# Projections of an attention layer: pair 0's operands put by in the pauses of the tiles, longer pauses, routing in smaller steps, two weight sums one product earlier

## The chip, the cores and the metric

The kernel runs on one core of a Trainium2 chip. The metric is the device time of one execution in microseconds (us), lower is better. The core has five engines that run side by side, each with its own queue: PE (matrix products), DVE (vector work), ACT (activations and copies), POOL (vector work without access to the matmul results) and SP, which here only issues DMA transfers. An engine takes its instructions in order: one that waits holds up everything queued behind it.

## The reference

Inputs are float32: hidden states x of 4 batches x 512 rows x 1024, attention weights w_qkv (1024 x 6144) and w_o (4096 x 1024), and the weights of a feed-forward part with routed low-rank additions.

```python
xn   = layernorm(x)
qkv  = xn @ w_qkv                        # 32 heads of 128, 8 key/value heads
attn = softmax(q k^T * D**-0.5 - slope * sqrt(distance), causal)
x = x + (attn v) @ w_o                   # attention
      + xn @ W.T + b                     # feed-forward
      + low_rank_r(xn) * weight          # ranks r = 8, 16, 32, 64; the best of 4 by a gate
# gate: probs = softmax(xn @ gate_w.T + gate_b); r = argmax(probs); weight = top / top
```

## The kernel before, in words

The big products are done by Strassen's scheme in Winograd's form, twice over: seven outer products i in the order 1, 2, 6, 3, 7, 4, 5 (`PROJECTED`), each of seven inner products m1 to m7 of four matmuls. That saves matmuls and costs sums: sums of activations, sums of weights, sums of results.

The change lies in `project()`, the first 580 us or so, which makes q, k and v. The batches form two pairs. The products are done in *sets*, each of 512 columns of w_qkv: a set of keys and values (kv) and two of queries (q, q), four times over for pair 0 (kv0, q0, q1, kv2, ... q7: 12 sets), then the same for pair 1. `item(st, i)` is one outer product of one set. Its inner products come in the order m1, m5, the m4 of the item before, m6, m3, m2, m7. Results are taken out of the matmul banks by DVE (L130), and some of them (of products 1 and 5) by copies on ACT (L168). Other work is spread between the inner products: after each of them `beside()` takes steps from queues of Python generators, and a generator's `yield` ends a step. The queues are

- `weights`: `outer_w`, the outer sums of a set's weights (L508; the record has them under the helper's line L133) on DVE. Three homes `to0`, `to1`, `to2` hold results; the rest is done in place.
- `soon`: sums of activations that are needed next.
- `later`: work with no near due time, one step every `pace[1]`-th inner product (4 at first, then 3, from the third set on 2). In order: a pause of 9 steps, `routing(0)`, `routing(1)`, seven `put_by` of pair 0, then eight `tile_of_second`, with `routing(2)` after the fourth and `routing(3)` after the eighth.
- `apart`: three generators `weights_put_by`, which prepare sums of the weights of later stages: ACT issues a load into a buffer `wr` (L757, L764), a pause of 8 steps, four sums on POOL or DVE, a pause of 4, then SP stores the buffer (L799).

`put_by(i)` (pair 0) stores the operands of outer product i to DRAM for a later stage: four stores s<-x of 256 KB (L451) and one s<-xi of 768 KB (L453), five steps for each i, 35 in all, all issued by SP. `tile_of_second(t)` treats 128 rows of the second pair: a load of x (L693), a pause of 5 steps, layernorm statistics on DVE (L255, L258, L262, L265) and the normalising on ACT (L260 table load, L266), transposes on PE (L271), a product with the low-rank and gate matrices, stores; for the second batch of the pair further loads (L719), a pause of 4 steps, and four sums. `routing(bi)` turns the gate's results of one batch into a mask, with DVE instructions of a few numbers a partition: the softmax (L300 to L311), the weight (L316, L317, L321), for each of three further ranks a maximum (L325, two of three), a comparison (L328) and a product (L329), then four products with the low-rank results (L333); after that PE transposes them (L346), POOL sets a row of ones (L348) and ACT copies them out.

PE and SP issue in a hand-written order throughout `project()` (`manual_schedule`), DVE and POOL from the fifth product of the second set (k == 1, i == 5) on; before that, and for ACT throughout, the framework's scheduler orders the instructions. At the end of product 1 of the last set of pair 0 (q7), `flush(later)` runs what is left in `later` at once, because from there on the activations of pair 1 take the places of pair 0 (`hand_over`).

Of the kernel before, what the change touches and what calls it, by code (L numbers as in the profile page):

```python
# [65 lines left out]
def kernel(  # L66
# [225 lines left out]
    def route(bi):  # L292
        u = us.pop(bi)
        shape = [P, NT, NR]

        def small(tag, n=NR):
            return stats.tile([P, NT, n], F32, tag=tag, name=f"{tag}_{bi}", bufs=1)

        lg, pr, red, inv, top = small("lg"), small("pr"), small("red", 1), small("inv", 1), small("top", 1)
        nc.vector.tensor_tensor(  # L300
            lg, u[:, :, RMAX:], gb.unsqueeze(1).to_broadcast(shape), ALU.add
        )
        nc.vector.tensor_reduce(red, lg, AX.X, ALU.max)
        nc.vector.tensor_tensor(lg, lg, red.to_broadcast(shape), ALU.subtract)
        nc.scalar.activation(pr, lg, AF.Exp)
        yield
        yield
        nc.vector.tensor_reduce(red, pr, AX.X, ALU.add)
        nc.vector.reciprocal(inv, red)
        nc.vector.tensor_tensor(pr, pr, inv.to_broadcast(shape), ALU.mult)  # L310
        nc.vector.tensor_reduce(top, pr, AX.X, ALU.max)  # L311


        yield
        wgt = small("wgt", 1)
        nc.vector.reciprocal(wgt, top)  # L316
        nc.vector.tensor_tensor(wgt, top, wgt, ALU.mult)  # L317


        msk, best = small("msk"), small("best", 1)  # L320
        nc.vector.tensor_copy(msk[:, :, 0:1], wgt)  # L321
        for s in range(1, NR):
            prev = pr[:, :, 0:1] if s == 1 else best
            if s > 1:
                nc.vector.tensor_tensor(  # L325
                    best, pr[:, :, 0:1] if s == 2 else best, pr[:, :, s - 1 : s], ALU.max
                )
            nc.vector.tensor_tensor(msk[:, :, s : s + 1], prev, top, ALU.is_lt)  # L328
            nc.vector.tensor_tensor(msk[:, :, s : s + 1], msk[:, :, s : s + 1], wgt, ALU.mult)  # L329
            yield  # L330
        lo = 0
        for s, hi in enumerate(RANKS):
            nc.vector.tensor_tensor(  # L333
                u[:, :, lo:hi],
                u[:, :, lo:hi],
                msk[:, :, s : s + 1].to_broadcast([P, NT, hi - lo]),
                ALU.mult,
            )
            lo = hi
        return u  # L340
# [11 lines left out]
    def project(attention):  # L352
# [5 lines left out]
        with pool("a") as sb, tc.tile_pool(name="stats", bufs=2, reuse_waits="tile") as stats:  # L358
# [137 lines left out]
            def outer_w(st):  # L496
                w = W[st]
                q = [w[:, i * HC : (i + 1) * HC, ts(j, HS)] for i in range(2) for j in range(2)]
                n = f"{st[1]}{st[0]}_{st[2]}"

                t = [buf(f"to{i}", f"to{i}_{n}") for i in ((1, 2, 0) if st == sets[1] else range(3))]
                t.insert(2, q[1])
                TO[st] = {3: q[3]}
                for i, k, u, v in (
                    (5, 0, q[1], q[0]), (6, 1, q[3], t[0]), (7, 2, q[3], q[1]), (4, 3, q[2], t[1])
                ):
                    for c in range(0, HC, 2):
                        sub(nc.vector, t[k][:, c : c + 2], u[:, c : c + 2], v[:, c : c + 2])  # L508
                        yield
                    TO[st][i] = t[k]  # L510

            def raw_w(st, i):
                w = W[st]
# [74 lines left out]
                )  # L588


            soon, later, weights = deque(), deque(), deque()
            apart = (deque(), deque(), deque())
            pace = [1, 4, 0, False, 0, 0]


            delayed = []
# [92 lines left out]
            def tile_of_second(t):  # L689

                bi, i = divmod(t - 2 * NT, NT)
                xr = flat(r4(f"xin_{t}"))
                nc.sync.dma_start(out=xr, in_=xf[:, t, :])  # L693
                yield from pause(5)
                yield from normalise(xr, xr, t)
                xn = xr
                yield
                yield
                xt = flat(r4(f"xt_{t}")).rearrange("p (c k) -> p c k", k=P)
                for half in range(2):  # L700
                    transposed(bank, xn, t, half, xt[:, half * HC : (half + 1) * HC, :])
                    yield
                yield
                low_rank(bank, t, lambda c: xt[:, c, :])

                def to(j, x):
                    nc.sync.dma_start(out=xo_d[j][:, :, ts(i, P)], in_=x)

                low, high = xt[:, :HC], xt[:, HC:]
                if bi == 0:  # L710
                    yield
                    to(1, low)
                    to(2, high)
                    yield
                    return

                xf_t = flat(r4(f"xb_{t}")).rearrange("p (c k) -> p c k", k=P)
                for j in range(2):
                    nc.sync.dma_start(  # L719
                        out=xf_t[:, j * HC : (j + 1) * HC], in_=xo_d[1 + j][:, :, ts(i, P)]  # L720
                    )
                to(4, high)
                yield from pause(4)
                add(V, high, low, high)
                yield
                sub(V, low, xf_t[:, :HC], low)
                yield
                sub(V, xf_t[:, :HC], high, xf_t[:, :HC])
                to(5, high)
                yield  # L730
                sub(V, xf_t[:, HC:], xf_t[:, HC:], xf_t[:, :HC])
                yield
                to(7, low)
                to(6, xf_t[:, :HC])
                yield
                to(3, xf_t[:, HC:])
                yield
# [69 lines left out]
            def pause(n):  # L807
                for _ in range(n):
                    yield

            def hand_over(a, b, i):


                soon.append(pause(2))
                soon.append(once(b.take, i))
                at = PROJECTED.index(i)
                if at:
                    soon.append(b.inner(PROJECTED[at - 1], V))
                if i == 5:
                    soon.extend([pause(6), b.inner(5, V)])  # L820
                    for j in OUTER:
                        later.append(b.put_by(j))
# [4 lines left out]
            def stream():  # L827
# [41 lines left out]
                for j in (3, 7, 4, 5):  # L869
                    if j in (3, 7):  # L870
                        soon.append(a.outer(j, (V, V, V, V)))
                    soon.append(a.inner(j, GP if j == 4 else V))
                later.extend(a.put_by(j) for j in OUTER)
                for t in range(2 * NT, 4 * NT):
                    later.append(tile_of_second(t))
                    if t % NT == NT - 1:
# [3 lines left out]
                for k, st in enumerate(sets):  # L880
                    if k + 1 < len(sets) and sets[k + 1] not in W:

                        in_while(4, lambda k=k: W.update({sets[k + 1]: load_w(sets[k + 1])}))
                    if k > 1:
                        weights.append(outer_w(st))
                    pace[5] = pace[2]

                    pace[1] = 3 if k < 3 else 2
                    for i in PROJECTED:
                        if k < 2 and i < 3:  # L890
                            continue
                        need(pairs[st[0]], i)
                        if i > 2:
                            need_w(st, i)
                        if k == 0 and i == 5:
                            weights.append(outer_w(sets[1]))

                        pace[3] = k > 0 and k not in (NS - 1, NS)

                        pace[4] = pace[2] + {1: 0, 5: 4}.get(i, 9)  # L900
                        if k == len(sets) - 1 and i == 3:
                            done_first.__exit__(None, None, None)
                            attention()
                        nxt = PROJECTED[PROJECTED.index(i) + 1 :][:1]
                        if nxt:
                            in_while(4, lambda st=st, j=nxt[0]: ahead(st, j))
                        elif k < len(sets) - 1:
                            in_while(4, lambda k=k: ahead(sets[k + 1], 1 if k else 6))
                        yield item(st, i, accs[st])
                        if k == NS - 1:  # L910
                            if i == 1:
                                flush(later)
                            hand_over(a, b, i)
                        if k == 1 and i == 5:
                            pace[0] = 1
                            in_order.__enter__()
                    del W[st], TO[st]
# [1 line left out]
            run(stream(), beside)  # L919
            release(0)  # L920
            in_order.__exit__(None, None, None)
            assert not (soon or later or weights or any(apart))


    def attend(front, begin):
# [737 lines left out]
```

## Time and profile before

| | |
|---|---|
| runs | 2672.40, 2672.93, 2676.59 us; median 2672.93 |
| profiled execution | 2674.55 us, of it the profile's span 2672.8 |
| mean granted clock of PE | 0.994 |
| PE busy | 2606.5 us (98%), 11872 matmuls |
| DVE busy | 1785.0 us (67%) |
| ACT busy | 651.9 us (24%) |
| POOL busy | 1921.2 us (72%) |
| DMA | 656.19 MB, mean 246 GB/s |

PE is busy 98% of the span, so what counts is where it stands still. The page gives the share of each engine; the chain that ended last is followed back from the last instruction to what released it. In a timeline each row has a start, a length, the engine, the line and the operation with the tile that it writes and those that it reads, and in brackets the engine's idle time before it with what ended it. In a table by stretches each engine's busy time stands with its count of instructions; PEclk is the clock that PE was granted and the DMA share is that of the core's 16 DMA engines (it can pass 1 where packets overlap).

### The profile page before, as it was taken

The page shows a single profiled execution, that of the slowest core. Times are in us where ns is not written, and L with a number is a line of the kernel's source. Part 1 is how long each engine was busy: PE and PEld are TensorE (multiplying, and loading weights), DVE is VectorE, ACT ScalarE, POOL GpSimd, SP SyncE. Part 2 cuts the span into 40 slices and gives each one's busy share as a digit, 9 for nine tenths or more (in the row PEclk, how much of TensorE's full clock was granted, in tenths as well). Part 3 has the DMA queues.
Part 4 walks back from the last instruction along what each step waited for, and adds up shares of the span by engine and source line. Part 5 has one row for each costly group of instructions (what it writes and reads, how often), then busy time and mean ns, then how long its engine had stood idle before and what let it go on. Part 6 is the DMA issues. An engine that isn't in the chain of part 4 may idle for free.

```text
span 2672.8 us, 36000 instructions
## 1 busy us (share of the span) xinstructions
PE 2606.5 (98%) x11872; PEld 2079.8 (78%) x11872; DVE 1785.0 (67%) x3646; ACT 651.9 (24%) x1730; POOL 1921.2 (72%) x1984
## 2 busy tenths in 40 slices
PE   7899999999999999999999999999999999999999
PEld 7787878888888888866666666665888888888887
DVE  6876676787676667566766666666665566656574
ACT  3011111100000000177666666675000000000000
POOL 2687787877888889667777778676675566756583
PEclk9999999999999999999999999999999999999999
DMA  4379777877976767336666565767987878878884
GB/s 138 105 264 357 240 259 259 289 241 273 316 245 217 257 217 263 121 112 207 224 202 226 188 227 190 229 225 231 356 282 282 300 295 321 294 276 313 303 315 162
DMA packets 386570, 656.19 MB, mean 246 GB/s; under 512 B 22441, under 2 KB 291113, under 8 KB 376274
## 3 DMA queue, kind: packets, MB, share of 16 engines
q1 hardware_dynamic: 314322, 566.47, 61.6%
q10 hardware_dynamic: 70752, 82.85, 9.5%
q0 software_dynamic: 1312, 4.59, 0.5%
q8 instruction: 95, 1.56, 0.2%
q14 instruction: 89, 0.73, 0.1%
HBM read 392.72 MB, written 261.10 MB: 245 GB/s over the span
## 4 chain that ended last, share of the span: by engine, by line
PE 68%; POOL 3%; DVE 3%; DMA 1%; issue 1%; SPq 0%; ACT 0%; ACTq 0%; POOLq 0%; DVEq 0%
PE pc L1263 14%; PE psc L996 10%; PE po L1034 10%; PE pd L1263 7%; PE pc_q L545 6%; PE ptr L1021 4%; PE pa L1263 4%; PE pc_kv L545 3%; PE pd_q L545 3%; PE pd_kv L545 2%; PE pa_q L545 1%; DVE pt L1024 1%; DVE p L1001 1%; PE pa_kv L545 1%; POOL ti_q L133 1%
## 5 line engine op out<-in xcount | busy, mean ns | idle before, releaser
L1010 POOL TENSOR_SCALAR p<-p,tot 128x256 f32<-128x256 f32 (+3 forms) x512 | 315.5, 635 | 131.6 <-DVE tot L1008 82.1
L1001 DVE CUSTOM_DVE_ANT_0 p<-psc,bias 128x256 f32<-128x256 f32 (+3 forms) x512 | 245.4, 491 | 96.7 <-PE psc L996 73.4
L996 PE MATMUL psc<-k,q 128*128 128x512 f32 (+3 forms) x1024 | 305.3, 437 | 1.4 <-ACT r_q L168 0.5
L1005 ACT ACTIVATE p<-p,low 128x256 f32<-128x256 f32 (+3 forms) x512 | 284.0, 555 | 70.2 <-DVE low L1001 58.1
L1034 PE MATMUL po<-pt,v 128*128 128x512 f32 x640 | 290.6, 592 | 0.0
L133 POOL TENSOR_TENSOR t<-w 128x640 f32<-128x640 f32 x95 | 181.5, 1910 | 135.7 <-DMA w<-m 61.3
L996 PEld LDWEIGHTS psc<-k,q 128*128 128x128 f32 x1024 | 172.8, 190 | 99.7 <-issue 55.0
L133 POOL TENSOR_TENSOR t<-w,t 128x640 f32<-128x640 f32 x95 | 196.7, 2070 | 40.8 <-PE pc L1263 37.0
L1021 PEld LDWEIGHTS ptr<-ident,p 128*128 128x128 f32 x1280 | 148.7, 142 | 77.3 <-issue 39.9
L1034 PEld LDWEIGHTS po<-pt,v 128*128 128x128 f32 x640 | 116.8, 190 | 108.5 <-issue 99.2
L133 POOL TENSOR_TENSOR wr<-wr 128x256 f32<-128x256 f32 x220 | 172.7, 787 | 27.3 <-DMA wr<-t 9.6
L1024 DVE COPY pt<-ptr 128x512 f32<-128x512 f32 x192 | 130.0, 684 | 82.3 <-PE ptr L1021 80.3
L1021 PE MATMUL ptr<-ident,p 128*128 128x128 f32 x1280 | 169.1, 276 | 9.9 <-DVE pt L1024 8.5
L545 PE MATMUL pc_q<-xi,ti_q 128*128 128x256 f32 x640 | 166.0, 382 | 5.0 <-DVE q L130 4.1
L133 POOL TENSOR_TENSOR ti_q<-w_q 128x256 f32<-128x256 f32 x128 | 104.6, 817 | 72.9 <-PE pc_kv L545 40.0
L168 ACT COPY m<-pc 128x256 f32<-128x256 f32 x30 | 11.2, 372 | 582.8 <-PE pc L1263 575.2
L133 DVE TENSOR_TENSOR wr<-wr 128x256 f32<-128x256 f32 x220 | 139.3, 633 | 13.1 <-DMA s<-xo 3.3
L545 PEld LDWEIGHTS pc_q<-xi,ti_q 128*128 128x128 f32 x640 | 119.9, 190 | 26.0 <-issue 5.2
L168 ACT COPY q<-pc_q 128x256 f32<-128x256 f32 x64 | 23.8, 372 | 395.0 <-PE pc_q L545 332.0
L545 PE MATMUL pd_q<-xi,ti_q 128*128 128x256 f32 x448 | 115.8, 381 | 3.9 <-POOL ti_q L133 3.9
L1263 PE MATMUL pc<-s,t 128*128 128x256 f32 x480 | 113.7, 385 | 4.1 <-DVE m L130 4.1
L1263 PE MATMUL pd<-s,w 128*128 128x256 f32 x480 | 113.2, 383 | 0.0
(337 smaller groups left out, 6013.3 us busy)
## 6 DMA issues: line engine op xcount, KB each, us to landing
sa<-s SPq DMA_DIRECT2D x98, 640.0 KB, 8.4
s<-ot SPq DMA_DIRECT2D x107, 384.0 KB, 5.4
m<-wr SPq DMA_DIRECT2D x70, 512.0 KB, 4.3
w<-m SPq DMA_DIRECT2D x28, 1280.0 KB, 6.7
w_q<-in_w_qkv_dram SPq DMA_DIRECT2D x16, 2048.0 KB, 12.9
q<-q SPq DMA_DIRECT2D x32, 1024.0 KB, 7.2
s<-os SPq DMA_DIRECT2D x45, 512.0 KB, 5.2
t<-wr SPq DMA_DIRECT2D x40, 512.0 KB, 4.5
```

What stands on the lines that cost most here:

```text
L133: return eng.tensor_tensor(dst, u, v, ALU.subtract)
L168: nc.scalar.copy(dst, src)
L545: nc.tensor.matmul(dst, ops_w[m][:, c, :], XI[i][m][:, c, :], start=start and c == 0, stop=c == 1, skip_group_check=True,)
L996: nc.tensor.matmul(sc[:, :n], Q[u][:, g, ts(i, P)], K[u][:, :n], start=True, stop=True)
L1001: nc.vector.tensor_tensor_reduce(pr[:, g], sc[:, :n], bias[p, h][:, g, S - n :], -SCALE, BIG, ALU.add, ALU.min, low,)
L1005: nc.scalar.activation(pr[:, g], pr[:, g], AF.Exp, bias=low, scale=-1.0, accum_out=tot[:, g : g + 1])
L1010: nc.gpsimd.tensor_scalar(pr[:, g], pr[:, g], tot[:, g : g + 1], 1.0, ALU.mult, ALU.mult)
L1021: nc.tensor.transpose(tr[:, ts(g, P)], PR[u, i][:, g, ts(j, P)], ident)
L1024: nc.vector.tensor_copy(pt, tr)
L1034: nc.tensor.matmul(po, V[u][:, j, :], PT[i, j], start=(j == 0), stop=(j == i))
L1263: nc.tensor.matmul(bk, w[:, k], x[:, k], start=start and k == 0, stop=stop and k == KB - 1, skip_group_check=True,)
```

## The change

Four edits, all in `project()` and `route`; every engine has as many instructions as before, in another order.

- Pair 0's `put_by` leaves `later` and goes into a queue of its own, `quiet`. A new generator `filled(n)` pauses n steps and takes a step from `quiet` in each. `tile_of_second` uses it: `filled(8)` in place of its pause of 5, `filled(6)` in place of the pause of 4.
- In the routing, the comparison (L328) and the product (L329) are in separate steps.
- In `outer_w`, the homes of the sums are taken when the sum is made. Set 1's homes change (its sums 5, 6 and 4 go to `to1`, `to2`, `to0`, as before, but one by one), its sums start at product 4 of set 0 and not at product 5; sums 5 and 6 are made there and the rest held until product 5 (`pace[6]`).
- `flush(quiet)` stands behind `flush(later)`.

```diff
@@ route @@
             nc.vector.tensor_tensor(msk[:, :, s : s + 1], prev, top, ALU.is_lt)
+            yield
             nc.vector.tensor_tensor(msk[:, :, s : s + 1], msk[:, :, s : s + 1], wgt, ALU.mult)
             yield
@@ outer_w @@
-                t = [buf(f"to{i}", f"to{i}_{n}") for i in ((1, 2, 0) if st == sets[1] else range(3))]
-                t.insert(2, q[1])
+                home = (1, 2, None, 0) if st == sets[1] else (0, 1, None, 2)
+                t = [None, None, q[1], None]
                 TO[st] = {3: q[3]}
                 for i, k, u, v in (
-                    (5, 0, q[1], q[0]), (6, 1, q[3], t[0]), (7, 2, q[3], q[1]), (4, 3, q[2], t[1])
+                    (5, 0, q[1], q[0]), (6, 1, q[3], 0), (7, 2, q[3], q[1]), (4, 3, q[2], 1)
                 ):
+                    v = t[v] if isinstance(v, int) else v
+                    if t[k] is None:
+                        t[k] = buf(f"to{home[k]}", f"to{home[k]}_{n}")
                     for c in range(0, HC, 2):
                         sub(nc.vector, t[k][:, c : c + 2], u[:, c : c + 2], v[:, c : c + 2])
                         yield
                     TO[st][i] = t[k]
+                    while st == sets[1] and i == 6 and not pace[6]:
+                        yield
@@ tile_of_second @@
-                yield from pause(5)
+                yield from filled(8)
...
-                yield from pause(4)
+                yield from filled(6)
@@ beside the other queues @@
+            def filled(n):
+                for _ in range(n):
+                    do(quiet)
+                    yield
@@ stream @@
-                later.extend(a.put_by(j) for j in OUTER)
+                quiet.extend(a.put_by(j) for j in OUTER)
...
-                        if k == 0 and i == 5:
+                        if k == 0 and i == 4:
                             weights.append(outer_w(sets[1]))
+                        pace[6] = k > 0 or i == 5
...
                             if i == 1:
                                 flush(later)
+                                flush(quiet)
```

More of the change, by code (lines that the diff above doesn't have):

```diff
@@ L588, in item @@
                 )
-            soon, later, weights = deque(), deque(), deque()
+            soon, later, weights, quiet = deque(), deque(), deque(), deque()
             apart = (deque(), deque(), deque())
-            pace = [1, 4, 0, False, 0, 0]
+            pace = [1, 4, 0, False, 0, 0, False]
             delayed = []
@@ L921, in project @@
             in_order.__exit__(None, None, None)
-            assert not (soon or later or weights or any(apart))
+            assert not (soon or later or weights or quiet or any(apart))
     def attend(front, begin):
```

## The prediction

> **What bounds the kernel now.** I read the page first, then the busy times by stretches of 50 us, then PE's waits between 100 and 700 us, then timelines around each stop of PE. The page:
>
> ```profile
> span 2672.8 us, 36000 instructions
> PE 2606.5 (98%) x11872; PEld 2079.8 (78%) x11872; DVE 1785.0 (67%) x3646; ACT 651.9 (24%) x1730; POOL 1921.2 (72%) x1984
> PE 68%; POOL 3%; DVE 3%; DMA 1%; issue 1%; SPq 0%; ACT 0%; ACTq 0%; POOLq 0%; DVEq 0%
> ```
>
> PE is the bound: 98% busy, 68% of the chain that ended last. The profiled execution took 2674.55 us (span 2672.8, 1.75 around it); the median of the runs is 2672.93 and they lie within 4.2 us. No instruction is added or removed on any engine, and behind 700 us the orders of both kernels agree, so only PE's stops in the projections can change. There are few:
>
> ```profile
> PE pc_q L545 <- DVE q L130: 4.1, 5, 1.7
> PE pc_kv L545 <- ACT kv L168: 3.2, 1, 3.2
> PE pc_q L545 <- DVE u_q L130: 2.0, 1, 2.0
> PE pd_q L545 <- POOL ti_q L133: 1.6, 2, 1.5
> PE pc_kv L545 <- DVE kv L130: 1.6, 2, 0.8
> PE pc_kv L545 <- DVE r_kv L130: 1.4, 1, 1.4
> ```
>
> (engine, operation and line; who was waited for; us, times, longest.) All waits of that stretch are some 19 us, 0.7% of the time; a difference of 0.2% (5.3 us) is about what a measurement of this kernel can tell from none, and bounds my chances.
>
> The largest stop stands at 235 us (start, length, engine, what, idle before and releaser):
>
> ```profile
> 226.06 1.62 SPq L799 DMA_DIRECT2D m<-wr  x1
> 232.89 1.78 ACTq L757 DMA_DIRECT2D wr<-in_w_o_dram  x2
> 234.77 0.37 ACT L168 COPY kv<-pc_kv 128x256 f32<-128x256 f32 x1 [5.66 <-issue]
> 235.29 2.05 PE L545 MATMUL pc_kv<-x,ti_kv 128*128 128x256 f32 x4 [3.18 <-ACT kv L168]
> 237.13 1.79 PE L545 MATMUL pc_q<-x,w_q 128*128 128x256 f32 x4
> 238.75 1.03 PE L545 MATMUL pd_q<-xi,ti_q 128*128 128x256 f32 x4
> ```
>
> PE waits for a copy on ACT; the copy stands behind ACT's issue of a weight load; that load refills a `wr` buffer which the store m<-wr must first have emptied. The sums for that store ended on POOL at 221.56, but SP issued it at 226.06, behind a row of s<-x stores of `put_by`, 1.2 to 4.4 us each. The stretch says why:
>
> ```profile
> core 0: us, PE busy (x) PEld busy (x) DVE busy (x) ACT busy (x) POOL busy (x), PEclk, DMA share, GB/s
> 200.00:250.00 50.00, 46.02 (x204) 39.36 (x203) 30.59 (x64) 2.98 (x8) 40.34 (x52) 0.97 1.05 371
> ```
>
> The DMA engines are full (1.05). PE then runs two groups of four matmuls in 2.05 and 1.79 us in place of 1.03: the clock dips after the stop.
>
> **The routing** is a chain of small DVE steps:
>
> ```profile
> 564.89 0.70 DVE L328 TENSOR_TENSOR msk<-pr,top 128x4 f32<-128x4 f32 x1
> 565.62 0.65 DVE L329 TENSOR_TENSOR msk<-msk,wgt 128x4 f32<-128x4 f32 x1
> 570.85 0.66 DVE L329 TENSOR_TENSOR msk<-msk,wgt 128x4 f32<-128x4 f32 x1
> 571.42 1.74 DVE L333 TENSOR_TENSOR us<-us,msk 128x32 f32<-128x32 f32 x4
> 569.92 1.13 PE L545 MATMUL pc_q<-x,ti_q 128*128 128x256 f32 x4 [0.79 <-DVE r_q L130]
> ```
>
> Four numbers a partition take 0.65 us here, but elsewhere the same L329 takes 0.17 (minimum, median, maximum 166/612/657 ns). The long ones end where an instruction of POOL ends; the four L333 took 0.61 at 375.33 while POOL did a memset, 2.17 at 122.12 beside POOL's sums.
> The Trainium skill ("GPSIMD Engine Reference", section 1, Specifications) says that GpSimd shares its SBUF interfaces with VectorE, in contention with instructions of two SBUF inputs; the trace agrees (0.17 against 0.65).
>
> **The change, part by part** (us of PE time, minus is faster; bounds in brackets).
>
> *Put-by of pair 0 out of `later`, into the tiles' pauses.* `later` loses 35 steps ahead of the tiles and gains 3 in each of eight tiles, 2 more in four, 3 in each of four routings: 32 + 12 - 35 = 9 steps more in all, one step every second product late. The first tile starts at about 195 us in place of 255. When POOL's sums of that store are done, some 8 s-stores have been issued and not 22, so the store and the load behind it should land in time. What goes: 3.18, the 0.80 stop at 225.82 (a load that took 5.79 to issue), and 1.7 of slow clock, 5.7 together; I take -5.0 (-5.7 to 0). The tile whose xin load was late at 255.40 (DVE idle 2.13, PE 1.24 at 256.56) loads in another place: -1.2 (-1.2 to 0). Stops at 394.31 (1.73), 398.56 (0.49) and 403.5 (0.23), a late `wr` load and a tile's statistics together: tiles move, loads remain, half goes, -1.2 (-2.4 to 0). At 443.91 and 446.32 (0.18, 0.28) a tile leaves: -0.5 (-0.5 to 0).
>
> *Set 1's weight sums one product up.* The 1.41 stop at 111.25 (DVE full with these sums at 104.7 to 111) goes. But the first sum writes home `to2`, which still holds set 0's sum for its product 4; DVE now waits there for PE's m2 of that product, and behind it on DVE's queue stands the eviction of m6, which PE's m7 needs. Eviction and sum (0.34 + 0.75) with 0.2 for the handover: 1.3 of new stop. Net -0.1 (-1.4 to +0.5).
>
> *A yield between L328 and L329.* A step shrinks from about 1.7 (L325 0.35, L328 0.65, L329 0.65) to 1.0 and 0.65. routing(0) loses 0.48 + 0.34 now, about 0.45 after: -0.4 (-0.8 to +0.5). routing(1) loses 2.04 at 151.70 and then 2.2 to the clock (products to 157.33 stretched); after, I count 2.3 in the same place and 0.9 where the four L333 meet q_1_7: -1.0 (-3.0 to +0.5).
>
> *routing(2)* moves from kv_4_7 and kv_4_4, products that leave DVE time (it lost 0.45 there), to kv_4_1 to kv_4_6, where DVE also has that set's weight sums. There the DVE is already full: from 339.04 to 352.3 it has no gap, and PE's eleven products lose 2.0. A tile's statistics (two L255 0.68, L258 0.19, L262 0.14, L265 0.21: 1.9) leave that stretch; three L329 (1.95), two L325 (0.7), two L328 (1.3) and the four L333 (1.5) come: 5.45. So 3.55 more on a full engine, all of it PE's, less the 0.45: +3.1. With the short rows (L329 0.17, L325 0.15, L328 0.61, L333 0.61: 2.6) it is 0.7 - 0.45, +0.3; with the steps L316 to L328 ahead of it (1.5) late too, +4.6. The displaced statistics meet evictions at q_6_2 and ACT's table load (1.28) meets copies at q_3_5 and q_5_1: +0.9 (0 to 2).
>
> *The flush.* With 9 steps more, routing(3) isn't done when product 1 of the last set (q_7) ends, where `flush(later)` empties the queue. Now the chain stands in one piece on DVE behind q_7_1's last eviction and a weight sum, fifteen instructions from L316 to L333, and PE's four transposes (L346) stand ahead of q_7_2's first product: PE has nothing to do until the last L333. Before, the chain was spread over 564.33 to 573.08 and cost 0.79 and 0.19. POOL has four ti sums left there (before: 578.48 to 581.8), then waits for PE. So the first six take their long rows: 0.17, 0.25, 0.17, 0.70, 0.65, 0.35, with 0.04 between, 2.5; one more L328 at 0.65, L329 0.17, L325 0.15, L328 0.61, L329 0.17, 1.75; L333 0.61. That is 4.9, near routing(2)'s chain (5.0). Ahead of it the eviction and the sum (0.41 + 0.88), and 0.6 of handovers and lateness: PE stands 6.8 us. With POOL idle throughout the chain is 3.1 (stop 5.0), with POOL busy throughout 7.05, routing(3)'s own (stop 9.0). Then the clock: after the stop of 3.61 at 82.41 the slow groups cost 3.1, after 3.18 1.7, after 2.04 2.2; mean 2.3. 6.8 + 2.3 - 0.98 = +8.1 (5.0 + 1.7 - 1.0 = +5.7 to 9.0 + 3.1 - 1.0 = +11.1).
> The Trainium skill ("TensorE: Matmul & The Clock Gate", Part 1) lets the clock fall to half after an idle window of about 3.4 us and rise after as long a busy one. Here a stop of 2.04 was enough, so the measurement decides; by the page the flush's tail would be an estimated 1.7 and the old stops' 3.9 of slow clock not theirs to give back, some 3 slower than my sum.
>
> **Sum.** Gains -5.0 - 1.2 - 1.2 - 0.5 - 0.1 - 0.4 - 1.0 = -9.4; losses +3.1 + 0.9 + 8.1 = +12.1; +2.7. On the profiled execution that is 2677.2, on the median 2675.6; I say 2676.5.
>
> **Rivals.** *S, slower:* the s-stores only change their place. Eight a tile, one every second product as before, now fall in 195 to 350 us, beside the 2 MB loads of weights (12.9 us each) and the `wr` loads. Should one burst again make a `wr` store late by over 4 us, the stop of 235 us comes back elsewhere with its slow clock (5.7 on top of 2676.5: 2682), and with the flush and routing(2) at their upper bounds (3.0 + 1.5 more) it is 2687. For it: stretches 250 to 350 have DMA shares of 0.85 and 0.73 without these stores. Against: a burst is a third of the old one. 0.25. *F, faster:* the stops by late transfers all go (5.7 + 1.2 + 2.4 + 0.5), routing(0) and set 1 give 0.5, routing(1) 3.0, together 13.3; routing(2) costs 0.3 by short rows, the flush 5.7 with POOL idle, the displaced statistics nothing: -7.3, 2666. For it: POOL waits whenever PE does. 0.17. *N, no net change:* pair 0's stores are only regrouped, the late ones stay late (5.0 not gained), and the flush hides behind work that POOL and DVE owe PE there anyway: -4.4 + 4.0 + some 0.5, 2673. Against: the order of the changed kernel has the chain whole and PE's transposes directly behind it. 0.10.
>
> **How the numbers follow.** My forecast has 0.48, its own range 2671 to 2682; above 2678.3 (0.2% over the median) lie some 0.17 of it, the rest within. S gives 0.25 to slower, F 0.16 to faster and 0.01 to the same, N 0.10 to the same. Faster 0.16, same 0.42, slower 0.42. The range leaves out half of F and half of S: 2667 to 2686.
>
> **What would show it.** Right: no wait of PE on an ACT copy at 235; a stop of PE of 5 to 9 us ahead of the four transposes L346 near 575, released by DVE L333, with stretched products after it; more DVE waits at kv_4_2 to kv_4_6; none at 111.25 but one some 5 us earlier. Wrong: PE passes the flush with under 3 us, or a new stop over 3 us on ACT or DMA between 195 and 350 us, or any difference behind 700 us.

## The result, and the profile after

The changed kernel takes 2667.43 us (median of 11 runs, 2666.04 to 2671.17) against 2672.93 (11 runs of the kernel before, 2669.29 to 2677.27). The ratio is 0.998, 95% interval 0.9972 to 0.9987: faster by 0.2%, some 5.5 us. The forecast was 2676.5, and the time lies just inside the range's low end, on the other side of no change. The profiled execution took 2668.48 us, its span 2666.7. The page of the changed kernel begins:

```profile
span 2666.7 us, 35998 instructions
PE 2601.2 (98%) x11872; PEld 2082.5 (78%) x11872; DVE 1787.2 (67%) x3646; ACT 650.7 (24%) x1730; POOL 1917.0 (72%) x1984
```

Each engine has the same number of instructions and about the same busy time. Line numbers moved: L545 is now L551, L329 is L330, L333 is L334, L346 is L347, L451 is L452, L757 is L763, L799 is L805. PE's waits between 100 and 700 us, the changed kernel (who waits, for whom: us, times, longest):

```profile
PE ptr_u L347 <- DVE us L334: 6.4, 1, 6.4
PE pc_kv L551 <- DVE kv L130: 2.4, 3, 1.5
PE pc_kv L551 <- DVE u_kv L130: 2.1, 2, 1.4
PE pd_q L551 <- POOL ti_q L133: 2.1, 3, 1.5
```

The wait for ACT's copy (3.2) is gone, the one for u_q fell from 2.0 to 0.4, and a new one of 6.4 heads the list: the flush. So a third of what PE now waits is one stop which the kernel before did not have, and the change still gains. The busy times by stretches of 50 us show where from:

```profile
200.00:250.00 50.00, 50.00 (x256) 44.40 (x256) 33.06 (x74) 8.71 (x18) 42.38 (x54) 1.00 0.95 328
250.00:300.00 50.00, 50.00 (x246) 44.31 (x245) 34.59 (x75) 5.68 (x13) 38.35 (x50) 1.00 0.98 335
550.00:600.00 50.00, 43.62 (x199) 37.95 (x198) 35.92 (x85) 4.47 (x10) 30.98 (x39) 0.93 0.58 184
```

(first after the stretch and its length: PE's busy time; the last three: PE's clock, DMA share, GB/s.) For 100 us PE does not stop at all, where it was busy 46.02 and 48.27 before, and from 550 to 600 it loses more than before (43.62 against 49.03). The DMA share of 200 to 250 fell from 1.05 to 0.95. At the place of the old stop, the changed kernel's timeline:

```profile
217.14 0.52 SPq L805 DMA_DIRECT2D m<-wr  x1
224.85 0.92 ACTq L763 DMA_DIRECT2D wr<-in_w_o_dram  x2
226.49 0.37 ACT L168 COPY kv<-pc_kv 128x256 f32<-128x256 f32 x1 [1.37 <-PE pc_kv L551]
```

SP issues the store when 11 stores of `put_by` have gone before it (27 in the kernel before, at 226.06), ACT issues two loads in 0.92 us together, and the copy waits only for PE, not "issue" for 5.66. The flush, PE and DVE:

```profile
559.33 0.87 DVE L133 TENSOR_TENSOR to_q<-w_q,to_q 128x512 f32<-128x512 f32 x1
561.59 0.57 DVE L330 TENSOR_TENSOR msk<-msk,wgt 128x4 f32<-128x4 f32 x1
563.35 0.17 DVE L330 TENSOR_TENSOR msk<-msk,wgt 128x4 f32<-128x4 f32 x1
564.20 1.03 PE L347 MATMUL ptr_u<-ident,us 128*64 128x128 f32 x4 [6.38 <-DVE us L334]
565.03 1.92 PE L551 MATMUL pc_q<-x,w_q 128*128 128x256 f32 x4
566.74 1.26 PE L551 MATMUL pd_q<-xi,ti_q 128*128 128x256 f32 x4
```

Eviction and weight sum first, then the chain: four of its first seven instructions (L316 to L328) are long, 0.48 to 0.66, beside POOL's sums; from 562.88 on, when POOL has only a memset left and then nothing, they are short (0.17). PE's first products after the stop take 1.92 and 1.26 in place of 1.03.

Along the span, the changed kernel stands against the one before, by the same stops of PE: 2.02 us earlier at 82.41 (80.39), 9.10 earlier at 620.15 (611.05), 8.72 at 683.69 (674.97), 5.70 at 716.06 (710.36), 6.07 at 2116.57 (2110.50). So 7.1 come from the stretch of the change. The 2.0 at the start vary from run to run: in the eleven profiles of this document the stop of 63.61 lies between 61.01 and 63.71, and the kernel without stores (below), whose order is that of before but for SP, has the earliest. The 3.0 given back between 684 and 716 are a dip of the clock: the same stop (1.51 + 0.29 here, 1.47 + 0.29 before) was followed by groups of 2.07 and 1.81 here and by full speed before; the rest is a stop of 0.38 for POOL at 689.95 and a longer wait for it (1.35 against 0.69).

### The profile page after: what moved, and what is told of

Same layout as the page of the kernel before. It is cut to its first block, busy times and chain, and to the rows that moved or that the text cites. A ratio compares the mean times of both kernels' runs of the same rounds, so it can differ in the third digit from the quotient of the medians.

```text
span 2666.7 us, 35998 instructions
## 1 busy us (share of the span) xinstructions
PE 2601.2 (98%) x11872; PEld 2082.5 (78%) x11872; DVE 1787.2 (67%) x3646; ACT 650.7 (24%) x1730; POOL 1917.0 (72%) x1984
## 4 chain that ended last, share of the span: by engine, by line
PE 67%; POOL 3%; DVE 3%; DMA 2%; issue 1%; SPq 1%; ACT 0%; POOLq 0%; DVEq 0%; ACTq 0%
PE pc L1277 14%; PE psc L1010 10%; PE po L1048 10%; PE pd L1277 7%; PE pc_q L551 6%; PE ptr L1035 4%; PE pa L1277 4%; PE pc_kv L551 3%; PE pd_q L551 3%; PE pd_kv L551 2%; PE pa_q L551 1%; DVE pt L1038 1%; DVE p L1015 1%; PE pa_kv L551 1%; POOL ti_q L133 1%
## 5 line engine op out<-in xcount | busy, mean ns | idle before, releaser
L551 PE MATMUL pc_q<-xi,ti_q 128*128 128x256 f32 x640 | 165.9, 382 | 1.6 <-DVE q L130 1.3
L551 PEld LDWEIGHTS pc_q<-xi,ti_q 128*128 128x128 f32 x640 | 121.2, 191 | 20.4 <-issue 3.4
L551 PE MATMUL pd_q<-xi,ti_q 128*128 128x256 f32 x448 | 116.1, 382 | 5.0 <-POOL ti_q L133 5.0
L133 POOL TENSOR_TENSOR ti_q<-to_q 128x256 f32<-128x256 f32 x96 | 75.6, 788 | 54.3 <-PE pc_q L551 43.9
```

What stands on the lines that cost most here:

```text
L133: return eng.tensor_tensor(dst, u, v, ALU.subtract)
L551: nc.tensor.matmul(dst, ops_w[m][:, c, :], XI[i][m][:, c, :], start=start and c == 0, stop=c == 1, skip_group_check=True,)
```

## The experiments

Theory: the row of s-stores made weight loads, and through ACT PE, late; the tiles' pauses take that away; the flush is a real cost. Rivals: the small steps of the routing, the earlier sums, or the longer pauses alone make the gain; PE owes the flush's time anyway.

**1. The tail without the longer pauses.** routing(3) then ends at q_6_7, ahead of the flush.

```diff
-                yield from filled(8)
+                yield from filled(8 if t < 3 * NT else 5)
...
-                yield from filled(6)
+                yield from filled(4)
```

> The changed kernel with the old pauses (5 and 4) in the last four tiles only, where the queue of put-by steps is empty after the first of them; routing(3) then ends before the flush, at q_6_7. Theory (the flush stands on the path: PE stopped 6.4 us for it and ran about 1.6 us of slow clock behind it): about 7 us under the changed kernel, 2660 to 2661, and no stop of PE on DVE L334. Rival (PE owes that time to something behind the flush, sums or loads that are late anyway): 2666 to 2668, with the stop moved to q_7_2 or later.

Measured 2669.65 (11 runs), ratio to the kernel before 0.9992 (0.9983 to 1.0001): no faster than the changed kernel, some 2 slower. The flush's stop is gone, but neither theory nor rival had it right: nothing moved to q_7_2; PE's waits on DVE for `q` grew to 3.5 (1.3 in the changed kernel), and new stops stand at 384 to 389 (1.75 in all), at 428 to 437 (2.61; the first two):

```profile
427.84 1.13 PE L551 MATMUL pc_q<-x,ti_q 128*128 128x256 f32 x4 [0.41 <-DVE u_q L130]
430.19 1.10 PE L551 MATMUL pc_q<-xi,ti_q 128*128 128x256 f32 x4 [1.22 <-DVE q L130]
```

at 477 to 480 (1.25) and 524 to 535 (2.86). On DVE there, a tile's sums stand between weight sums:

```profile
427.71 0.88 DVE L133 TENSOR_TENSOR to_q<-w_q,to_q 128x512 f32<-128x512 f32 x1
428.51 1.21 DVE L133 TENSOR_TENSOR xt<-xb,xt 128x512 f32<-128x512 f32 x1
```

In the sets from q_4 to q_6 of the changed kernel, DVE has two of a set's weight sums (128x512) on product 1, three on 2, two on 6, one on 3 and none on 7 and 4. In the changed kernel the last four tiles' sums lie on products 6, 3, 7 and 4; with the short pauses nearly all of them lie on products 1 and 2, and routing(3) falls on q_6_2 to q_6_7. The new theory: what counts is the product on which a tile's DVE work falls, and the longer pauses moved it.

**2. The yield alone, on the kernel before.** Only the added `yield`; later has 12 more steps, so routing(3) meets the flush here too.

> The kernel before with nothing but the yield between comparison and product; it adds 12 steps to the queue, so routing(3) falls into the flush here too, with the put-by where it was. Theory (small steps give 2 to 3 us at routing(0) and routing(1), the flush costs 6.4 + 1.6 - 1.0 = 7): 2676 to 2678, slower than before, and the stop at 235 us still there. Rival (the small steps are what made the changed kernel faster): 2667 to 2669.

Measured 2683.95 (5 runs), ratio 1.0046 (1.0033 to 1.0059): slower, by more than expected. The small steps did their part: in place of 0.48, 0.34 and 2.04 with a dip there are 0.31, 0.68 and 0.70. The flush stands (7.78, and two slow groups behind it), and so do ACT's copy (2.12 at 229.63, behind two loads whose issue took 1.76 together) and a new wait for POOL with a dip at 260.77 (2.93). Beyond the forecast are also a stop of 1.22 with a dip at 434.05, on q_5_2 among a tile's sums, and one of 1.27 at 527.92.

**3. The put-by and the pauses, without the yield and the sums.**

> The kernel before with the put-by in the tiles' pauses and the longer pauses, and neither the yield nor the earlier weight sums; routing(3) ends before the flush (q_6_5). Theory (the row of s-stores made weight and tile loads late: 5.7 at 225 to 238, 1.2 at 256, some 1.6 of the 2.4 at 394 to 403): 2664 to 2665. Rival (moving stores gives nothing without the small steps): 2672 to 2674.

Measured 2669.19 (11 runs), ratio 0.9993 (0.9984 to 1.0002). The stops at 225, 235 and 256 are gone, as the theory had it, but the time is 4 to 5 us above the theory's. New stops stand in other places: 1.93 at 269.28, a tile's transposes behind ACT's normalising, with two slow groups; 1.04 at 302.38; 2.40 with a dip at 388.97; 3.1 in three stops at 437 to 445; 1.35 at 498.56. Without the yields the tiles stand on other products, with their sums beginning on product 1 of q_4, 2 of q_5, 6 of kv_6 and 3 of q_6.

**4. The kernel before without pair 0's stores.** `put_by` keeps its 35 steps for pair 0 and issues nothing.

```diff
-                        nc.sync.dma_start(out=d[:, slot], in_=src)
+                        if self.p:
+                            nc.sync.dma_start(out=d[:, slot], in_=src)
                         yield
-                    nc.sync.dma_start(out=d[:, 4:7], in_=self.T[i][:, :3])
+                    if self.p:
+                        nc.sync.dma_start(out=d[:, 4:7], in_=self.T[i][:, :3])
```

> The kernel before with pair 0's 35 s-stores left out and every step kept in its place, so the order of all engines stays but for SP; the last stage reads pair 1's operands in place of pair 0's for those rows, in 49 loads split in two (the result of pair 0 is not the reference's). Theory (the stores' transfers and their issue on SP are what made the loads late): the stops at 225, 235 and 256 go, 7 us: 2665 to 2667. Rival (the loads are late for their place in the order, not for the stores): 2672 to 2674 with the stop on ACT's copy still there.

Measured 2662.61 (5 runs), ratio 0.9965 (0.9953 to 0.9978). With DVE, POOL and PE in the old order, the stops at 225, 235 and 256 are gone, while those that no transfer causes stay, at 1.41, 0.48, 0.34 and 2.04. So the stores and not the place of the loads made them. The run takes out both the stores' issue on SP and their transfers, so it does not tell which of the two made the loads late. PE's waits between 100 and 700 us of this kernel, with no wait for ACT's copy and 2.6 for `q` where it was 4.1:

```profile
PE pd_q L547 <- POOL ti_q L133: 2.9, 3, 1.4
PE pc_q L547 <- DVE q L130: 2.6, 4, 1.0
PE pc_q L547 <- DVE u_q L130: 2.0, 1, 2.0
PE pc_kv L547 <- DVE r_kv L130: 1.4, 1, 1.4
```

The 10 us are more than the 7 expected. From start to start of PE's groups (explained below) the two profiles differ by 9.9 between the stops at 82 and 620 us: 6.1 at 225 to 238, 1.5 at 256, 0.4 at 394 to 403 (1.73 at 394 fell to 1.04), and some 1.9 in small stops elsewhere.

**5. A later flush.** The queue `quiet` is flushed where it was, `later` four products on.

```diff
                             if i == 1:
-                                flush(later)
                                 flush(quiet)
+                            if i == 7:
+                                flush(later)
```

> The changed kernel with the flush of the queue later moved from the end of product 1 of q_7 to the end of its product 7; the put-by queue is still flushed at product 1. routing(3) then runs in steps through q_7_1, q_7_2 and q_7_6, beside weight sums, and every tile keeps its place. Theory (the flush is 6.4 of stop and some 1.6 of slow clock on the path; the spread chain costs 2 to 3 among weight sums, as at kv_4_1 to kv_4_6): 2661 to 2663. Rival (PE is owed that time anyway; the first run without the flush was no faster): 2667 to 2669.

Measured 2661.09 (5 runs, 2658.12 to 2662.39), ratio to the kernel before 0.9953 (0.9941 to 0.9966), 6.3 under the changed kernel: the low end of the theory's range. The chain, in steps among weight sums, leaves two listed stops:

```profile
559.88 1.13 PE L551 MATMUL pd_q<-xi,ti_q 128*128 128x256 f32 x4 [0.24 <-POOL ti_q L133]
562.92 1.13 PE L551 MATMUL pd_q<-xi,w_q 128*128 128x256 f32 x4 [0.17 <-DVE q L130]
```

The flush was on the path, nothing stood behind it, and the chain in steps costs less than the 2 to 3 that I had given it (0.41 of listed idle, 1.0 from start to start).

**6. The tiles' sums ten products earlier**, all else in its place (a tile is as long as before).

```diff
-                yield from filled(6)
+                yield from filled(1)
...
                 to(3, xf_t[:, HC:])
                 yield
+                yield from pause(5)
```

> The changed kernel with the pause ahead of the four sums of a tile of the last batch cut from 6 to 1 and 5 steps of pause put behind them: the same length of a tile, statistics, stores and routing in the same place, the sums 10 products earlier. Three of them then fall on q_4_2, one on q_5_2, where DVE has weight sums. Theory (what counts is on which product of a set a tile's DVE work falls): 2.6 of stop at q_4_2, as in the run with short pauses, and under 1 at q_5_2, less 0.8 that they cost where they were: 2669 to 2670. Rival (place in the set does not matter, the length of the pauses does): 2667 to 2668.

Measured 2672.75 (11 runs), ratio 0.9996 (0.9987 to 1.0005), 5.3 over the changed kernel. At q_4_2 and q_4_6, where the sums now stand, PE stops 1.64, 0.50, 0.54 and 0.49 between 384 and 392, 0.54 at 443.76 and 0.88 at 492.62; the changed kernel has 0.40 and 0.40 at 392 and 394. The listed stops between 90 and 600 us are 16.8 against 13.4, and the clock stayed slow a group longer behind the flush, whose stop was shorter (5.63 against 6.38), so that stop and slow clock together cost the same. So the place decides, as in the first run; its size was put too low by half.

**7. The old weight sums, all else as changed.**

> The changed kernel with the weight sums of the second set as they were (from product 5, homes taken at once). Theory (one stop is exchanged for another, 1.46 at 100 for 1.41 at 110): 2667 to 2668, no difference. Rival (the earlier sums are part of the gain, for DVE is less late for the routing behind them): 2669 to 2670.

Measured 2667.41 (11 runs), ratio to before 0.9977 (0.9968 to 0.9986): the changed kernel's time. 1.41 at 109.25 stands in place of 1.46 at 100.42.

**8. The put-by in the pauses at their old length.**

> The kernel before with the put-by in the tiles' pauses at their old length (5 and 4), no yield, old weight sums. Five stores a tile and not eight, over seven tiles; tiles' sums at product 2 and 6 of their sets (kv_4, q_4, q_5, kv_6), routing(2) at q_3_2. Theory (the stores' relief of 7 to 10 is there, but collisions of tiles and routing with weight sums take most of it): 2668 to 2671. Rival (the stores alone make the gain; the longer pauses only delay): 2663 to 2665.

Measured 2669.17 (11 runs), ratio 0.9984 (0.9975 to 0.9993), as the theory had it. No stop over 0.2 is left between 160 and 290 us, and eleven of 0.5 to 1.1 stand between 299 and 504 (the longest, 1.07 at 373.58, waits for a copy behind ACT's normalising of a tile), where routing(2) lies on q_3_2 to q_3_3 and tiles' sums on products 2 and 6.

**9. The changed kernel without pair 0's stores**, left out as in the fourth run.

> The changed kernel with pair 0's 35 s-stores left out and their steps kept, as the same was done to the kernel before (the last stage reads pair 1's operands in their place; the result of pair 0 is not the reference's). Theory (in the tiles' pauses the stores cost PE nothing, since no stop between 170 and 300 us is left): 2666 to 2668, no difference to the changed kernel. Rival (the stores still cost, as the 10 us in the kernel before are more than its stops at 225, 235 and 256 explain, 7): 2662 to 2664.

Measured 2666.62 (11 runs), ratio to before 0.9986 (0.9977 to 0.9995), 0.8 under the changed kernel and within its spread. In the pauses the stores cost next to nothing; before they cost 10.

## Why the prediction was wrong

The forecast was +2.7 us on the profiled execution; between the same stops at 82.41 and 620.15 the changed kernel is 7.1 faster, 9.8 from the forecast. Most mechanisms were those of the text, and their sizes were wrong, nearly all to the same side. Both profiles hold the same 2449 matmuls between those stops, so the places can be compared by the starts of PE's groups: a group of four takes 0.86 us from start to start at full clock, and what a place takes beyond that is lost. A stop loses some 0.27 more than the idle time that the view lists: around the one of 0.40 at 394.23, groups start at 392.80 and 395.20, 2.40 for two groups and not 1.73. PE time lost, changed kernel less kernel before, us:

| step | forecast | shown |
|---|---|---|
| late `wr` store, 225 to 238 | -5.0 | -6.1 (no stop from 170 to 308) |
| late xin load at 256 | -1.2 | -1.5 |
| stops at 394 to 403 | -1.2 | -2.0 (3.4, now 1.3) |
| stops at 444 and 446 | -0.5 | -1.4 (with one at 441 that the view does not list) |
| set 1's weight sums | -0.1 | +0.3 (1.7, now 1.7 and 0.3 at 109.30) |
| routing(0) | -0.4 | -1.3 (no stop left) |
| routing(1) | -1.0 | -2.0 (4.5, now 2.5: stops of 0.30, 0.69 and 0.70, no dip) |
| routing(2) among weight sums | +3.1 | +1.2 (3.8 against 2.1 + 0.5) |
| displaced statistics, ACT's table | +0.9 | +1.0 (0.4 at 418.82, 0.6 at 520.23) |
| the flush | +8.1 | +6.5 (8.0: stop 6.5, slow clock 1.5; before 1.5) |
| slow clock behind 82.41 | 0 | -0.2 |
| small stops not forecast | 0 | -1.5 |
| sum | +2.7 | -7.0 (-7.1 before rounding) |

**The step that failed.** No one term makes up the 9.8. The largest is the costing of routing(2), its small instructions at their long rows on a full engine ("So 3.55 more on a full engine, all of it PE's"): +3.1 forecast, +1.2 shown. PE stops there, at kv_4_2 and kv_4_6, mostly twice:

```profile
331.36 1.13 PE L551 MATMUL pc_kv<-x,ti_kv 128*128 128x256 f32 x4 [1.36 <-DVE u_kv L130]
339.61 1.13 PE L551 MATMUL pc_kv<-x,ti_kv 128*128 128x256 f32 x4 [1.17 <-DVE c_kv L130]
```

I had counted 5.45 for routing(2) between the weight sums. It took 4.3, the sum of its rows from 326.6 to 338.1, some at 0.15:

```profile
332.02 0.15 DVE L330 TENSOR_TENSOR msk<-msk,wgt 128x4 f32<-128x4 f32 x1
333.90 0.15 DVE L325 TENSOR_TENSOR best<-best,pr 128x4 f32<-128x4 f32 x1
334.09 0.17 DVE L328 TENSOR_TENSOR msk<-best,top 128x4 f32<-128x4 f32 x1
338.08 1.15 DVE L334 TENSOR_TENSOR us<-us,msk 128x32 f32<-128x32 f32 x4
```

POOL was itself waiting at 332 and 334 (1.02 and 0.69 idle, for DVE), so it was not there to lengthen them. The chain also began before the first weight sum and used 1.62 of idle time that DVE had there before. The Trainium skill ("GPSIMD Engine Reference", section 1) has GpSimd contend with VectorE's instructions of two SBUF inputs; these rows agree, 0.15 with POOL idle and 0.68 for the same L330 at 326.60 beside a sum of POOL.

The second is the size of the gains. The stops by late transfers all went or shrank, -11.0 in the first four rows where I had taken -7.9, part of it by halving and rounding down, part because I took most gains at the listed idle time, some 0.27 a stop too little. For routing(1) I kept 0.9 for the four L333 and 2.3 at the old place, and gave back only 1.0. Split in two, the step never made PE stop over 0.70, so the dip of 2.2 fell away with it.

The third is the clock behind the flush, 1.5 where I had taken the mean of three dips, 2.3; and the spread chain had cost 1.5 by the starts, not 0.98.

Two readings of the text were wrong without deciding anything. The load "that took 5.79 to issue" is one row of the view for two loads, issued in 0.44 and 0.37 us at 217.99 and 223.40; the stores of "1.2 to 4.4 us each" include a row of three (4.36), of which the longest took 1.69.

Right were the flush (a stop of 6.38 where I had 6.8, released by L334, with slow groups behind it), the exchange of stops in the second set, the displaced statistics, the late store at 235 and its cure, and that nothing behind the projections changes in order. Rival S, a burst that moves the stop, did not come: there is no stop between 168.37 and 308.77. Rival F came nearest: its sum (-7.3, 2666) is about what was measured, but it had 9.8 for the late transfers, 3.0 for routing(1), nothing for the displaced statistics and none of the small stops, so that its total agrees is partly luck.

That the parts depend on each other I had not seen. The yield alone is 11 us slower and the put-by with the longer pauses alone is not clear of no change; together they are faster (the seventh run has both and is at the changed kernel's time). My text treated the longer pauses as nine steps of delay, while they decide on which product of a set a tile's sums fall.

## What to carry to other kernels

A queue of stores that runs ahead of an urgent store on the same issuing engine can cost through the buffer that the urgent one frees (here 10 us, and next to nothing once the stores were spread): look at which load waits for it, and who stands behind that load's issue. Work spread by a counter over a periodic schedule has a phase: a change in the number of steps moves everything behind it onto other places, so read the order that comes out, place by place, and expect single parts to lose what the whole gains. Where a queue is flushed at a fixed point, check what is still in it; moving that point four products on was worth more than the whole change.

## What the runs showed that I had not expected

- The same stop may or may not be followed by a slow clock. 2.04 us at routing(1) was, in each of the four kernels that have it; 1.51 + 0.29 at 675 us was here and 1.47 + 0.29 was not before; a stop of 5.63 in the sixth run had groups of 1.91, 1.91 and 1.31 behind it, one of 6.38 only 1.92 and 1.26. In all eleven profiles the slow stretches between 70 and 720 us last 3.4 or 6.8 us, and within a run they start whole multiples of 3.41 us apart. On that grid, a stretch at full clock was followed by a slow one when PE stood for 1.80 us or more of it, and not when it stood for 1.73 or less, with one exception (1.63 in the second run at 431 to 434.4). So it counts how a stop falls on the grid. The two stops at 675 and 683 us, the changed kernel first (PE's busy time after the length, then PEld, DVE, ACT, POOL, and PE's clock third from the end):

```profile
673.00:676.40 3.40, 1.60 (x8) 0.74 (x6) 1.19 (x3) 0.00 (x0) 3.24 (x5) 1.00 1.03 386
676.40:679.80 3.40, 3.40 (x8) 2.78 (x9) 2.54 (x5) 0.00 (x0) 2.91 (x5) 0.50 1.04 357
682.30:685.70 3.40, 1.72 (x7) 1.22 (x8) 1.44 (x4) 0.00 (x0) 3.32 (x5) 1.00 1.05 402
685.70:689.10 3.40, 3.40 (x18) 2.99 (x16) 3.29 (x7) 0.00 (x0) 3.32 (x6) 1.00 1.05 357
```

  The Trainium skill ("TensorE: Matmul & The Clock Gate", Part 1) says that the window that the clock's gate watches runs freely; the grid and the spread behind equal stops agree with that, while dips after 2 us of stop lie below its idle window of 3.4.
- A DVE instruction on four numbers a partition takes 0.15 to 0.17 us with POOL idle or at a memset, and up to 0.77 (at 112.74) beside a sum of POOL, then ending 0.02 to 0.03 us after it. One that starts within the last 0.1 us of such a sum can be short too (0.15 at 561.40), so its price is set by what the other engine is doing at that moment.
